# A four-layer attention and Mamba kernel: normed input in both partition halves, the Silu one step later, and layer 1 in half-unit steps

## The chip, the cores and the metric

The kernel runs on one core of a Trainium2 chip, everything in float32. The metric is the device time of one execution in microseconds (us), the median of three runs. The core has a matrix engine (TensorE, PE in the profile, with its weight loads shown apart as PEld), and VectorE (DVE), ScalarE (ACT) and GpSimd (POOL) for elementwise work. SyncE (SP) only issues DMA transfers. Each engine works through its own instructions in program order, and semaphores tie the engines together.

## What is computed

The input is 2 images of 64 channels and 96 x 96 pixels. Four layers follow each other; with two images of 64 channels, the 128 partitions hold image 0 in rows 0 to 63 and image 1 in rows 64 to 127.

- Layer 0 is self-attention over all 9216 pixels, with 1x1 convolutions around it.
- Layer 1 is a depthwise and a 1x1 convolution, then one Mamba block along each image's 9216 pixels as a single sequence.
- Layer 2 is four Mamba blocks: forward and backward along the columns, then forward and backward along the rows, each sequence 96 long.
- Layer 3 is a 3x3 filter whose taps depend on the image's mean.

The change concerns layers 1 and 2. A Mamba block, cut to what matters:

```python
hn = normed(seq)                                  # layer norm (layer 1), RMS norm (layer 2), over 64 channels
xm, z = split(hn @ in_proj_w.T)                   # 64 -> 128 and 128
xc = silu(causal_conv(xm, 4 taps) + convd_b)
dt, Bm, Cm = split(xc @ x_proj_w.T)               # 4, 16, 16
dt = softplus(dt @ dt_proj_w.T + dt_proj_b)
dA = exp(dt[..., None] * A)                       # 128 channels x 16 states
dBx = dt[..., None] * Bm[:, :, None, :] * xc[..., None]
h = h * dA + dBx                                  # along the sequence
y = einsum('bds,bs->bd', h, Cm)
out = ((y + xc * Dp) * silu(z)) @ out_proj_w.T
```

## The kernel before

Work is cut into units of 768 pixels (CH = 768, HALF = 384). Layer 1 has 24 units, 12 per image, one after the other with a carried state; layer 2 has 96, of 8 whole sequences each, a forward and a backward unit sharing one normed input. A unit has 128 channels x 16 states = 2048 recurrences, and they are laid out as 16 groups of 8 channels x 16 states, 128 rows each. So every unit has 16 steps. The rows of dt and of dt*x are written to DRAM and read back, each row repeated, into a tile `spread`.

In layer 1 a step is one group over the whole unit; in layer 2 (`paired`) it is two groups over half of the unit:

```python
    def paired(self, step):
        half, m = divmod(step, self.STEPS // 2)
        return half, (2 * m, 2 * m + 1)
    ...
    def inputs(self, u, step):                     # dt*x*B, VectorE
        if not u.paired:
            u.bx = self.places[0][1]
            self.nc.vector.tensor_mul(u.bx, u.dtu[step][:, CH:], u.B)               # L872
            return
        bx = self.places[step % 2][1].rearrange("p (q t) -> p q t", q=2)
        ...
        B = self.low[0].unsqueeze(1).to_broadcast([P, 2, HALF])
        self.nc.vector.tensor_mul(bx, x, B)                                          # L877

    def scan(self, u, step):                       # VectorE, then GpSimd
        h = u.h[step]
        if not u.paired:
            first = u.carry[:, step : step + 1]
            nc.vector.tensor_tensor_scan(h, h, u.bx, first, ALU.mult, ALU.add)       # L884
            nc.gpsimd.tensor_copy(first, h[:, CH - 1 :])                             # L885
            nc.gpsimd.tensor_mul(h, h, u.C)                                          # L886
            return
        ...
        nc.vector.tensor_tensor_scan(h[:, way], h[:, way], bx[:, way], 0.0, ...)     # L890
        nc.gpsimd.tensor_mul(h, h, C.unsqueeze(1).to_broadcast([P, 2, HALF]))        # L893

    def gather(self, u, step):                     # TensorE: sum over the states, into y
        ...
        if begin:
            ... matmul(p, lhsT=u.w.direct, rhs=u.xc[...], start=True, stop=False)    # L907
        for i, (_, p, q, n) in enumerate(parts):
            ... matmul(p, lhsT=self.t.gather[n], rhs=h[...], start=False, stop=stop) # L910
```

`read` issues the transfer into `spread` five steps ahead (six buffers), `decay` (L853 in layer 1, L857 in layer 2, ScalarE) makes dA three steps ahead, and `shared` (L866, TensorE) puts B of the next unit or half into PSUM: at step 6 for the second half and at step 14 for the next unit. In layer 2, PSUM has one bank for B and one for y, so `y_half` (L915) must copy the first half's sums out at mid-unit before L907 may start the second.

The products of the 64 normed channels use only the rows of one image:

```python
    def conv(self, u, half):                       # L748 in layer 1, L754 in layer 2
        rows = rows_of(u.b)
        x = u.norm.x[rows]
        ...
        for j in range(D_CONV):
            lhsT = u.w.taps[rows, D_CONV - 1 - j]
            ... matmul(p, lhsT=lhsT, rhs=x[:, ...], ...)

    def gate_mm(self, u):
        rows = rows_of(u.b)
        u.p = self.mm([(u.w.gate_w[rows], self.halves(u.norm.x[rows, D_CONV - 1 :]))])

    def gate_read(self, u):
        self.nc.scalar.copy(u.gate, u.p)                                             # L772
        self.nc.scalar.activation(u.raw, u.raw, AF.Silu)                             # L773, with a table load
        self.nc.scalar.preload_act_table_set("natural_log_exp_and_others")           # L774, the load back
```

`mm` is a helper of one line, so that norm, gate, dt, C and output products all stand at L666. Everything apart from the step itself is a piece with an offset in steps relative to its unit; pieces of several units run side by side:

```python
    PIECES = (
        (-51, "norm_centre"), (-49, "norm_square"), (-47, "norm_mean"), (-45, "norm_root"),
        (-38, "norm_scale"), (-36, "norm_affine"),
        (-27, "conv_0"), (-26, "conv_1"), (-25, "conv_read"), (-25, "gate_mm"), (-23, "gate_read"),
        (-21, "step_mm"), (-19, "step_read"), (-18, "step_exp"), (-17, "step_kept"), (-17, "step_log"),
        (-17, "c_mm"), (-15, "c_read"), (-15, "step_sum"), (-11, "step_dt"), (-9, "step_u"), (-8, "step_write"),
        (10, "y_half"), (18, "y_read"), (19, "y_gate"), (25, "tail_0"), (26, "tail_1"), (27, "tail_read"),
    )
```

In each step the main loop gives out: read, decay, inputs and scan, shared, gather of two steps before, then the pieces of that step, those named in `reads` first. `step_kept`, `step_sum`, `step_dt` and `step_u` are products and sums of GpSimd, `step_write` is the transfer of dt and dt*x to DRAM (L824).

Of the kernel before, what the change touches and what calls it, by code (L numbers as in the profile page):

```python
# [25 lines left out]
P = 128  # L26
# [3 lines left out]
NB = 512  # L30
# [41 lines left out]
def setup(ctx, tc, x, cols, mats, dtw):  # L72
# [32 lines left out]
    for b in range(B):  # L105
        nc.vector.memset(k.mean_c[rows_of(b), rows_of(b)], 1.0 / C)
    k.eps = const.tile([P, 1], FP, name="eps")
# [416 lines left out]
def mamba_tables(k, pool):  # L524
# [23 lines left out]
    t.centre = pool.tile([P, P], FP, name="centre")  # L548
    nc.vector.tensor_sub(t.centre, k.ident, k.mean_c)
# [64 lines left out]
class Mamba:  # L614
# [19 lines left out]
    def __init__(self, k, tables, wk, dram, ps, ps_m):  # L634
        self.k, self.nc, self.t = k, k.nc, tables
        self.wk, self.dram, self.ps_m = wk, dram, ps_m


        self.places = [self.wide(ps.tile([P, 2 * NB], FP, name=f"place{i}")) for i in range(2)]
        self.low = [ps.tile([P, NB], FP, name=f"low{i}")[:, :HALF] for i in range(2)]  # L640
# [40 lines left out]

    def norm_centre(self, u):
        if u.carry:
            rows = rows_of(u.b)
            u.p = self.mm([(self.t.centre[rows, rows], self.halves(u.image))], rows)

    def norm_square(self, u):  # L690
        if u.norm.unit is not u:
            return
        rows = rows_of(u.b)
        u.norm.x = self.work("xn", D_CONV - 1 + CH)
        u.sq = self.work("sq", bufs=1)[rows]
        if u.carry:
            self.nc.scalar.activation(u.sq, u.p, AF.Square)
            self.nc.scalar.copy(u.norm.x[rows, D_CONV - 1 :], u.p)
        else:
            n = u.image.shape[1]  # L700
            self.nc.scalar.activation(u.sq.rearrange("p (n t) -> p n t", n=n), u.image, AF.Square)

    def norm_mean(self, u):
        if u.norm.unit is u:
            rows = rows_of(u.b)
            u.p = self.mm([(self.k.mean_c[rows, rows], self.halves(u.sq))], rows)

    def norm_root(self, u):
        if u.norm.unit is u:
            self.nc.scalar.activation(u.sq, u.p, AF.Ln, bias=self.k.eps[rows_of(u.b)])  # L710
            self.nc.scalar.activation(u.sq, u.sq, AF.Exp, scale=-0.5)

    def norm_scale(self, u):
        if u.norm.unit is not u:
            return
        nc, rows = self.nc, rows_of(u.b)
        x = u.norm.x[rows, D_CONV - 1 :]
        if u.carry:
            before = u.norm.x[rows, : D_CONV - 1]
            if u.norm.before is None:  # L720
                nc.gpsimd.memset(before, 0.0)
            else:
                nc.gpsimd.tensor_copy(before, u.norm.before.x[rows, CH:])
            nc.gpsimd.tensor_mul(x, x, u.sq)
        else:
            split = lambda t: t.rearrange("p (n t) -> p n t", n=u.image.shape[1])
            nc.gpsimd.tensor_mul(split(x), u.image, split(u.sq))

    def norm_affine(self, u):
        if u.carry:  # L730
            rows = rows_of(u.b)
            x = u.norm.x[rows, D_CONV - 1 :]
            self.nc.scalar.activation(x, x, AF.Identity, bias=self.k.col("ln_b", rows), scale=self.k.col("ln_g", rows))
# [3 lines left out]
    def conv(self, u, half):  # L737
        rows = rows_of(u.b)
        x = u.norm.x[rows]
        if half == 0:  # L740
            u.sides, u.p = self.open("conv")
        p = u.sides[half]
        c0 = D_CONV - 1 + half * HALF
        for j in range(D_CONV):
            lhsT = u.w.taps[rows, D_CONV - 1 - j]
            flags = dict(start=j == 0, stop=j == D_CONV - 1)
            if u.carry:
                self.nc.tensor.matmul(p, lhsT=lhsT, rhs=x[:, c0 - j : c0 + HALF - j], **flags)  # L748
                continue
            p3 = p.rearrange("p (n t) -> p n t", t=W)  # L750
            x3 = x[:, c0 : c0 + HALF].rearrange("p (n t) -> p n t", t=W)
            late, early = slice(j, W), slice(0, W - j)
            o, i = (early, late) if u.rev else (late, early)
            self.nc.tensor.matmul(p3[:, :, o], lhsT=lhsT, rhs=x3[:, :, i], **flags)  # L754

    def conv_0(self, u):
        self.conv(u, 0)

    def conv_1(self, u):
        self.conv(u, 1)  # L760
# [6 lines left out]
    def gate_mm(self, u):  # L767
        rows = rows_of(u.b)
        u.p = self.mm([(u.w.gate_w[rows], self.halves(u.norm.x[rows, D_CONV - 1 :]))])

    def gate_read(self, u):
        self.nc.scalar.copy(u.gate, u.p)  # L772
        self.nc.scalar.activation(u.raw, u.raw, AF.Silu)  # L773
# [8 lines left out]
    def step_read(self, u):  # L782
# [3 lines left out]
        order = "p (j a t) -> p a j t" if u.paired else "p (a j t) -> p a j t"  # L786
        both = u.both.rearrange(order, a=2, j=2)
# [47 lines left out]
    def paired(self, step):  # L835
        half, m = divmod(step, self.STEPS // 2)
        return half, (2 * m, 2 * m + 1)

    def read(self, u, step):
        u.dtu[step] = self.work("spread", 2 * CH, bufs=6)  # L840
        if not u.paired:
            self.nc.sync.dma_start(out=u.dtu[step], in_=u.rows[8 * step : 8 * step + P])
            return
        half, groups = self.paired(step)
        for q, n in enumerate(groups):
# [3 lines left out]
    def decay(self, u, step):  # L849

        h = u.h[step] = self.work("h", bufs=9)
        if not u.paired:
            self.nc.scalar.activation(h, u.dtu[step][:, :CH], AF.Exp, scale=u.w.rates[:, step : step + 1])  # L853
            return
        for q, n in enumerate(self.paired(step)[1]):
# [3 lines left out]
    def shared(self, u, half=0):  # L859

        if u.paired:
            sides, halves = [self.low[0]], [half]
        else:
            (sides, u.B), halves = self.places[1], range(2)
        for j, p in zip(halves, sides):
            self.nc.tensor.matmul(p, lhsT=u.w.bc[0], rhs=u.xc[:, bass.ts(j, HALF)], start=True, stop=True)  # L866

    def inputs(self, u, step):

        if not u.paired:  # L870
            u.bx = self.places[0][1]
            self.nc.vector.tensor_mul(u.bx, u.dtu[step][:, CH:], u.B)  # L872
            return
        bx = self.places[step % 2][1].rearrange("p (q t) -> p q t", q=2)
        x = u.dtu[step].rearrange("p (q a t) -> p q a t", q=2, a=2)[:, :, 1]
        B = self.low[0].unsqueeze(1).to_broadcast([P, 2, HALF])
        self.nc.vector.tensor_mul(bx, x, B)  # L877

    def scan(self, u, step):
        nc = self.nc  # L880
        h = u.h[step]
        if not u.paired:
            first = u.carry[:, step : step + 1]
            nc.vector.tensor_tensor_scan(h, h, u.bx, first, ALU.mult, ALU.add)  # L884
            nc.gpsimd.tensor_copy(first, h[:, CH - 1 :])  # L885
            nc.gpsimd.tensor_mul(h, h, u.C)  # L886
            return
        bx = self.places[step % 2][1]
        way = slice(None, None, -1) if u.rev else slice(None)
        nc.vector.tensor_tensor_scan(h[:, way], h[:, way], bx[:, way], 0.0, ALU.mult, ALU.add)  # L890
        h = h.rearrange("p (q t) -> p q t", q=2)
        C = u.C[:, bass.ts(self.paired(step)[0], HALF)]
        nc.gpsimd.tensor_mul(h, h, C.unsqueeze(1).to_broadcast([P, 2, HALF]))  # L893

    def gather(self, u, step):

        if u.paired:
            half, groups = self.paired(step)
            parts = [(half, self.low[1], q, n) for q, n in enumerate(groups)]
            begin, end = step % 8 == 0, step % 8 == 7  # L900
        else:
            parts = [(j, p, j, step) for j, p in enumerate(self.low)]
            begin, end = step == 0, step == self.STEPS - 1
        h = u.h[step]
        if begin:
            for half, p in {half: p for half, p, _, _ in parts}.items():
                self.nc.tensor.matmul(p, lhsT=u.w.direct, rhs=u.xc[:, bass.ts(half, HALF)], start=True, stop=False)  # L907
        for i, (_, p, q, n) in enumerate(parts):
            stop = end and (i == 1 or not u.paired)
            self.nc.tensor.matmul(p, lhsT=self.t.gather[n], rhs=h[:, bass.ts(q, HALF)], start=False, stop=stop)  # L910

    def y_half(self, u):
        if u.paired:
            u.y = self.work("yg")
            self.nc.scalar.copy(u.y[:, :HALF], self.low[1])  # L915

    def y_read(self, u):
        if u.paired:
            self.nc.scalar.copy(u.y[:, HALF:], self.low[1])
        elif not u.drained:  # L920
            u.y = self.work("yg")
            for j, p in enumerate(self.low):
                self.nc.scalar.copy(u.y[:, bass.ts(j, HALF)], p)
# [20 lines left out]
    def tail_read(self, u):  # L944
# [19 lines left out]
        (-27, "conv_0"),  # L964
        (-26, "conv_1"),
        (-25, "conv_read"),
        (-25, "gate_mm"),
        (-23, "gate_read"),
        (-21, "step_mm"),
# [20 lines left out]
    def lates(now, s):  # L990
        halves = now and now[0].paired
        if s == 2 or (s == 10 and halves):
            return ()
        if s == 3 or (s == 11 and halves):
            return (3, 2)
        return (2,)

    def run(self, units, first, n_first, other):


        for u in units:
            u.dtu, u.h, u.paired, u.drained = {}, {}, not u.carry, False
        steps = [(u, s) for u in units for s in range(self.STEPS)]
        at = lambda n: steps[n] if 0 <= n < len(steps) else None
        reads = ("norm_square", "norm_root", "conv_read", "gate_read", "step_read", "c_read", "tail_read")

        table = [[] for _ in range(self.STEPS)]
        unit = lambda i: units[i] if i < len(units) else None
# [16 lines left out]
        for n in range(begin, len(steps) + end + 1):  # L1025
# [5 lines left out]
            if at(n):  # L1031
# [3 lines left out]
                if not u.paired:  # L1035
# [318 lines left out]
```

## Time and profile before

| | before |
|---|---|
| time, median of 3 runs | 8185.35 us (8180.19 to 8186.09) |
| span of the profiled execution | 8174.9 us |
| mean granted TensorE clock | 0.955 |
| instructions | 80364 |
| layer 1, first scan to last scan | 2753.5 to 3935.3 us |
| layer 2, first scan to last scan | 3944.0 to 8091.7 us |
| DMA moved | 1725.90 MB |

The first line of the page gives each engine's busy time and its share of the span. A group line gives source line, engine, operation, tile written and tiles read, shapes, count, then busy time and mean nanoseconds of one, then the idle time of that engine just before and what ended most of it. A line of waits names who waited for whom, the total in us, the number of times and the longest. In a timeline each line has the start, the duration, the engine and the source line; square brackets hold the idle time before it. Matmul records come two to a float32 product.

### The profile page before, as it was taken

Reading aid. Unit: us, or ns where it says so; the run is one execution under the profiler, and the core shown is the slowest. Engines: PE = TensorE matmul, PEld = TensorE weight load, DVE = VectorE, ACT = ScalarE, POOL = GpSimd, SP = SyncE. Lnnn points to the kernel's source line nnn. Section 1 sums busy time; section 2 is a strip of 40 time slices with the busy share of each in tenths; the row PEclk is TensorE's granted clock in tenths of the full one; section 3 lists DMA queues with packets and bytes.
Section 4 is the critical chain, followed back from the end, with each engine's and each line's share of the span. In section 5 each row is a group of like instructions: output and inputs, shape, how many; then the busy total and the mean of one; then the engine's idle time right before and its main releaser. Section 6 shows DMA issues by size and latency. Waiting matters only on the chain.

```text
span 8174.9 us, 80364 instructions
## 1 busy us (share of the span) xinstructions
PE 7554.5 (92%) x24578; PEld 3358.0 (41%) x24578; DVE 6785.6 (83%) x5136; ACT 5045.4 (62%) x6473; POOL 4755.1 (58%) x3146
## 2 busy tenths in 40 slices
PE   9999999999999799999889998989999999999897
PEld 3333333333333344444444444444444444444443
DVE  6666666666666599988899999999999999999999
ACT  4444444444444566665676677777777777777774
POOL 0000000000000588888888888898999989888895
PEclk9999999999999798988999999999999999999999
DMA  1000000000000588777888888888898888888885
GB/s 42 1 1 1 1 1 1 3 4 4 4 4 5 205 294 296 284 286 277 292 315 317 317 321 333 330 324 331 334 337 328 330 336 336 331 321 334 324 329 211
DMA packets 538496, 1725.90 MB, mean 211 GB/s; under 512 B 59844, under 2 KB 60996, under 8 KB 537544
## 3 DMA queue, kind: packets, MB, share of 16 engines
q1 hardware_dynamic: 536608, 1717.66, 56.8%
q8 instruction: 194, 3.18, 0.2%
q10 hardware_dynamic: 1448, 3.05, 0.1%
q14 instruction: 246, 2.02, 0.1%
HBM read 1522.68 MB, written 197.79 MB: 210 GB/s over the span
## 4 chain that ended last, share of the span: by engine, by line
PE 21%; POOL 13%; issue 12%; ACT 8%; DMA 8%; DVE 4%; SPq 0%; DVEq 0%; ACTq 0%; POOLq 0%
PE low L910 10%; DMA spread<-rows 6%; POOL h L886 5%; POOL h L893 4%; PE mm L666 4%; ACT h L857 4%; PE conv L754 4%; DVE place L877 2%; DMA rows<-dtu 1%; PE low L907 1%; PE conv L748 1%; DVE h L890 1%; POOL dtu L811 1%; PE low L866 1%; ACT raw L773 1%
## 5 line engine op out<-in xcount | busy, mean ns | idle before, releaser
L910 PE MATMUL low<-h,pair 128*128 128x384 f32 x7680 | 2865.4, 515 | 44.2 <-POOL h L886 26.5
L893 POOL TENSOR_TENSOR h<-h,C 128x768 f32<-128x768 f32 x1536 | 2755.1, 1819 | 231.7 <-DVE h L890 225.1
L890 DVE TENSOR_TENSOR_SCAN h<-h,place 128x768 f32<-128x768 f32 x1536 | 2604.3, 1737 | 4.9 <-ACT h L857 4.9
L910 PEld LDWEIGHTS low<-h,pair 128*128 128x128 f32 x7680 | 1503.2, 201 | 1288.6 <-issue 270.7
L307 ACT ACTIVATE e<-f_exp 128x1536 f32<-128x1536 f32 x864 | 1207.1, 1449 | 1223.7 <-PE f_exp L297 1223.7
L363 DVE TENSOR_TENSOR acc_e<-acc_e,e 128x1536 f32<-128x1536 f32 x792 | 1389.9, 1755 | 684.5 <-ACT e L307 645.2
L857 ACT ACTIVATE h<-spread,xa 128x384 f32<-128x384 f32 x3072 | 1717.2, 607 | 368.7 <-DMA spread<-rows 336.8
L877 DVE TENSOR_TENSOR place<-spread,low 128x768 f32<-128x768 f32 x1536 | 1388.3, 949 | 251.0 <-PE low L866 238.4
L336 POOL TENSOR_TENSOR xa<-xa,t_att 64x512 f32<-64x512 f32 x36 | 45.4, 1261 | 2612.4 <-ACT t_att L334 2612.4
L314 PE MATMUL y_att<-e,xb 128*64 128x512 f32 x5184 | 1243.6, 601 | 0.0
L297 PE MATMUL f_exp<-theta,phi 64*128 64x512 f32 x5184 | 1234.4, 606 | 1.0 <-DVE xb L280 0.5
L297 PEld LDWEIGHTS f_exp<-theta,phi 64*128 64x128 f32 x5184 | 466.2, 186 | 754.6 <-issue 460.8
L884 DVE TENSOR_TENSOR_SCAN h<-h,state,place 128x768 f32<-128x768 f32 x384 | 696.1, 1813 | 67.7 <-ACT h L853 19.2
L886 POOL TENSOR_TENSOR h<-h,C 128x768 f32<-128x768 f32 x384 | 695.3, 1811 | 31.4 <-POOL state L885 1.0
L314 PEld LDWEIGHTS y_att<-e,xb 128*64 128x64 f32 x5184 | 341.5, 136 | 830.7 <-issue 829.3
L765 ACT ACTIVATE raw<-conv,cols 128x768 f32<-128x768 f32 x120 | 108.2, 901 | 886.1 <-PE conv L754 587.0
L754 PE MATMUL conv<-xn,xa 64*128 64x384 f32 (+3 forms) x1536 | 557.9, 503 | 16.6 <-DVE xa L1128 5.3
L872 DVE TENSOR_TENSOR place<-spread,place 128x768 f32<-128x768 f32 x384 | 369.1, 961 | 129.3 <-PE place L866 116.9
L853 ACT ACTIVATE h<-spread,rates 128x768 f32<-128x768 f32 x384 | 351.1, 931 | 175.0 <-DMA spread<-rows 173.6
L907 PE MATMUL low<-raw,xa 128*128 128x384 f32 x384 | 220.2, 662 | 257.8 <-ACT yg L915 175.6
L754 PEld LDWEIGHTS conv<-xn,xa 64*128 64x128 f32 x1536 | 277.6, 190 | 286.7 <-issue 98.7
L805 POOL TENSOR_TENSOR kept<-dtu,kept 128x768 f32<-128x768 f32 x120 | 218.2, 1819 | 285.1 <-ACT kept L798 285.1
(207 smaller groups left out, 6041.4 us busy)
## 6 DMA issues: line engine op xcount, KB each, us to landing
spread<-rows SPq DMA_DIRECT2D x3072, 384.0 KB, 6.4
spread<-rows SPq DMA_DIRECT2D x384, 768.0 KB, 4.5
rows<-dtu SPq DMA_DIRECT2D x240, 768.0 KB, 5.8
image<-pre SPq DMA_DIRECT2D x11, 384.0 KB, 2.3
xb<-image SPq DMA_DIRECT2D x11, 384.0 KB, 7.9
xa<-in_x SPq DMA_DIRECT2D x1, 2304.0 KB, 22.2
out<-xa ACTq DMA_DIRECT2D x7, 240.0 KB, 2.0
out<-xa SPq DMA_DIRECT2D x1, 1200.0 KB
```

Source lines behind the costliest of these rows:

```text
L297: nc.tensor.matmul(fs[j // 3][:, bass.ts(j % 3, NB)], lhsT=phi[at, bass.ts(m // 2, P)], rhs=theta[at, bass.ts(i, NB)], start=True, stop=True,)
L307: nc.scalar.activation(e, f, AF.Exp)
L314: nc.tensor.matmul(y[rows_of(m % 2)], lhsT=g[:, m, :], rhs=es[j // 3][:, bass.ts(j % 3, NB)], start=m < 2, stop=m >= KEYS - 2,)
L363: nc.vector.tensor_add(acc, acc, e)
L754: self.nc.tensor.matmul(p3[:, :, o], lhsT=lhsT, rhs=x3[:, :, i], **flags)
L857: self.nc.scalar.activation(h[:, bass.ts(q, HALF)], dt, AF.Exp, scale=u.w.rates[:, n : n + 1])
L877: self.nc.vector.tensor_mul(bx, x, B)
L884: nc.vector.tensor_tensor_scan(h, h, u.bx, first, ALU.mult, ALU.add)
L886: nc.gpsimd.tensor_mul(h, h, u.C)
L890: nc.vector.tensor_tensor_scan(h[:, way], h[:, way], bx[:, way], 0.0, ALU.mult, ALU.add)
L893: nc.gpsimd.tensor_mul(h, h, C.unsqueeze(1).to_broadcast([P, 2, HALF]))
L910: self.nc.tensor.matmul(p, lhsT=self.t.gather[n], rhs=h[:, bass.ts(q, HALF)], start=False, stop=stop)
```

## The change

The normed input, until now in the 64 rows of its own image, is made twice, in rows 0 to 63 and 64 to 127. With that, a product over 64 rows can take the first half of the unit from the lower rows and the second half from the upper ones, so that the two sides lie next to each other in the array's rows, each in its own PSUM bank. This concerns the mean, the conv and the gate. Second, the Silu with its two table loads becomes a piece of its own, one step after the gate's copy, and `y_half` moves to the front of its step. Third, layer 1 takes the half-unit steps of layer 2: two groups over half of the unit, each scan cut in two because the two groups have different carried states. The branches on `paired` go away.

```diff
-    t.centre = pool.tile([P, P], FP, name="centre")
-    nc.vector.tensor_sub(t.centre, k.ident, k.mean_c)
+    t.centre = pool.tile([P, 2, C], FP, name="centre")
+    for j in range(2):
+        nc.vector.tensor_add(t.centre[:, j], k.ident[:, :C], k.ident[:, C:])
+        nc.vector.tensor_scalar_add(t.centre[:, j], t.centre[:, j], -1.0 / C)
...
-        self.low = [ps.tile([P, NB], FP, name=f"low{i}")[:, :HALF] for i in range(2)]
+        self.B, self.y = [ps.tile([P, NB], FP, name=name)[:, :HALF] for name in ("B", "y")]
...
+    def mm_split(self, lhsT, rhs):
+        sides, whole = self.open()
+        for j, p in enumerate(sides):
+            at = rows_of(j)
+            self.nc.tensor.matmul(p, lhsT=lhsT[at], rhs=rhs[at, bass.ts(j, HALF)], start=True, stop=True)
+        return whole
...
     def norm_centre(self, u):
         if u.carry:
-            u.p = self.mm([(self.t.centre[rows, rows], self.halves(u.image))], rows)
+            u.p = self.mm([(self.t.centre[rows_of(u.b)], self.halves(u.image))])
...
     def norm_square(self, u):
...
         else:
-            n = u.image.shape[1]
-            self.nc.scalar.activation(u.sq.rearrange("p (n t) -> p n t", n=n), u.image, AF.Square)
+            for j in range(2):
+                self.nc.scalar.copy(x[rows_of(j)].rearrange("p (n t) -> p n t", n=u.image.shape[1]), u.image)
+            self.nc.scalar.activation(u.sq, x, AF.Square)
...
-            u.p = self.mm([(self.k.mean_c[rows, rows], self.halves(u.sq))], rows)
+            u.p = self.mm_split(self.k.mean, u.sq)
...
-    def conv(self, u, half):
...
+    def conv(self, u):
+        sides, u.p = self.open("conv")
         for j in range(D_CONV):
...
+            for half, p in enumerate(sides):
+                at = rows_of(half)
+                x, lhsT = u.norm.x[at], u.w.taps[at, D_CONV - 1 - j]
...
     def gate_mm(self, u):
-        u.p = self.mm([(u.w.gate_w[rows], self.halves(u.norm.x[rows, D_CONV - 1 :]))])
+        u.p = self.mm_split(u.w.gate_w, u.norm.x[:, D_CONV - 1 :])
 
     def gate_read(self, u):
         self.nc.scalar.copy(u.gate, u.p)
+
+    def silu(self, u):
         self.nc.scalar.activation(u.raw, u.raw, AF.Silu)
         self.nc.scalar.preload_act_table_set("natural_log_exp_and_others")
...
     def scan(self, u, step):
...
+        half, turns = self.turns(step)
+        h, bx = u.h[step], self.places[step % 2][1]
+        h2 = h.rearrange("p (q t) -> p q t", q=2)
+        if u.carry:
+            state = u.carry[:, turns[0] : turns[1] + 1]
+            for q in range(2):
+                at = bass.ts(q, HALF)
+                nc.vector.tensor_tensor_scan(h[:, at], h[:, at], bx[:, at], state[:, q : q + 1], ALU.mult, ALU.add)
+            nc.gpsimd.tensor_copy(state.unsqueeze(2), h2[:, :, HALF - 1 :])
+        else:
...
+        nc.gpsimd.tensor_mul(h2, h2, u.C[:, bass.ts(half, HALF)].unsqueeze(1).to_broadcast([P, 2, HALF]))
...
-        (-27, "conv_0"),
-        (-26, "conv_1"),
+        (-27, "conv"),
         (-25, "conv_read"),
         (-25, "gate_mm"),
         (-23, "gate_read"),
+        (-22, "silu"),
         (-21, "step_mm"),
...
-        reads = ("norm_square", "norm_root", "conv_read", "gate_read", "step_read", "c_read", "tail_read")
+        reads = ("y_half", "norm_square", "norm_root", "conv_read", "gate_read", "step_read", "c_read", "tail_read")
```

The cut parts are the other side of each `paired` branch, the same rows in `norm_scale` and `norm_affine`, and the main loop without its cases for layer 1. The 1x1 products, the attention of layer 0 and layer 3 stay as they are.

## The prediction

> **What bounds the kernel now.** I read the page first, then the waits, then the timeline of VectorE (DVE) in the middle of layer 2, then the busy time by stretch. The page shows no single full engine:
>
> ```profile
> PE 7554.5 (92%) x24578; PEld 3358.0 (41%) x24578; DVE 6785.6 (83%) x5136; ACT 5045.4 (62%) x6473; POOL 4755.1 (58%) x3146
> ```
>
> That is an average over four stages. The scans tell the stages apart: L884 (layer 1) first starts at 2753.5 us, L890 (layer 2) runs from 3944.0 to 8091.7 us. So attention takes 2.65 ms, layer 1 (24 units of 16 steps) 1190 us or 49.6 us a unit, layer 2 (96 units) 4149 us or 43.2 us a unit, and the end 82 us. The diff leaves attention and layer 3 alone, so only 5.34 ms can move. The costliest groups there:
>
> ```profile
> L910 PE MATMUL low<-h,pair 128*128 128x384 f32 x7680 | 2865.4, 515 | 44.2 <-POOL h L886 26.5
> L893 POOL TENSOR_TENSOR h<-h,C 128x768 f32<-128x768 f32 x1536 | 2755.1, 1819 | 231.7 <-DVE h L890 225.1
> L890 DVE TENSOR_TENSOR_SCAN h<-h,place 128x768 f32<-128x768 f32 x1536 | 2604.3, 1737 | 4.9 <-ACT h L857 4.9
> ...
> L877 DVE TENSOR_TENSOR place<-spread,low 128x768 f32<-128x768 f32 x1536 | 1388.3, 949 | 251.0 <-PE low L866 238.4
> ```
>
> DVE never waits for its scan, but it waits 251 us before the products L877, nearly all of it for L866, the two matmuls that put the next B in PSUM. The DVE timeline shows what it does when nothing holds it, and what one hold costs:
>
> ```profile
> 5005.81 3.39 DVE L890 TENSOR_TENSOR_SCAN h<-h,place 128x768 f32<-128x768 f32 x2
> 5012.80 1.83 DVE L877 TENSOR_TENSOR place<-spread,low 128x768 f32<-128x768 f32 x2 [3.60 <-PE low L866]
> 5014.54 3.39 DVE L890 TENSOR_TENSOR_SCAN h<-h,place 128x768 f32<-128x768 f32 x2
> 5017.85 1.80 DVE L877 TENSOR_TENSOR place<-spread,low 128x768 f32<-128x768 f32 x2
> 5019.56 3.39 DVE L890 TENSOR_TENSOR_SCAN h<-h,place 128x768 f32<-128x768 f32 x2
> ```
>
> From scan pair to scan pair is 5014.54 to 5019.56, 5.02 us for two steps, so a unit can't be shorter than 8 x 5.02 = 40.1 us, while it takes 43.2. Why is L866 late? PE takes its matmuls in order, and the waits show what stands ahead of it:
>
> ```profile
> DVE place L877 <- PE low L866: 238.4, 99, 5.2
> ...
> PEld low L907 <- ACT yg L915: 205.8, 49, 4.3
> PE low L907 <- ACT yg L915: 175.6, 49, 3.7
> ```
>
> L915 is y_half, ScalarE's copy that empties the single y bank at mid-unit; L907 is the first matmul into it afterwards. In the whole timeline L774 (the second table load of the Silu) runs 4999.16 to 5000.44, two decays follow, y_half runs at 5001.48, and L907 starts at 5001.99 after PE idled 3.71 us. PE then works without a break until L866 at 5011.96. The Silu block on ScalarE (load 1.28, Silu 1.48, load 1.28 = 4.04 us) therefore reaches DVE through PE. PE cannot catch up soon, as it is nearly full, and so are the others:
>
> ```profile
> 6000.00:7000.00 1000.00, 908.18 (x2526) 467.02 (x2526) 944.71 (x750) 724.33 (x1136) 900.65 (x529) 0.95 0.89 333
> 7000.00:8000.00 1000.00, 906.15 (x2511) 463.93 (x2509) 937.86 (x746) 722.64 (x1124) 892.17 (x524) 0.95 0.88 328
> ```
>
> (Columns: PE, weight loads, DVE, ACT, POOL busy; clock; DMA share; GB/s.) Per unit of 43.2 us: PE 39.2, DVE 40.7, ACT 31.3, POOL 38.7, DMA 38.2.
>
> **What the skill says.** "TensorEngine Tiling (Array Packing)", section Key Properties: different tiles of the array can load and multiply at the same time, and a change of the tiling mode drains the array. This trace agrees with the first: attention's 64-row scores L297, which alternate between the row halves, cost 1234.4/5184 = 238 ns for 512 columns, 0.47 ns a column, against 2865.4/7680 = 373 ns for 384 columns, 0.97 ns a column, for full-height L910. The timeline also shows some 0.55 us of PE idle where it turns to a 64-row product. "TensorE: Matmul & The Clock Gate", section The mechanism (what overlaps): matmuls keep program order, which is what the chain above needs. "ScalarE: Activation LUTs", section What ACT_TABLE_LOAD costs: 1283 ns and a drain of some 1380 ns. The load is 1283 ns here as well, but Silu follows it at once (5038.71 plus 1.28, next start 5040.01), so I count no drain.
>
> **The change part by part.**
>
> *Side-by-side products.* The conv L754 is 16 matmul records a unit, 557.9/96 = 5.8 us. Its two sides now sit in different row halves and different banks, alternately in program order; by the L297 ratio that halves: 2.9 us saved. The gate (192.0 us for 120 units, 1.6 us each) saves 0.8; the mean (121.9 us for 72 norms, 1.7 us each) saves 0.85 per norm, 0.4 per layer 2 unit. Sum 4.1 us of PE per unit, 39.2 to 35.1. In layer 1 the conv L748 costs 190.5/24 = 7.9, so 4.0 + 0.8 + 0.85 = 5.6 us.
>
> *Both halves filled.* In layer 2 one strided 64-row Square (1198 ns) becomes two such copies (my estimate 1.2 us each, same shape) and a plain Square (0.8): +2.0 us of ACT per norm, 1.0 per unit. Off the path unless ACT is late there. POOL's norm product goes from 1997 to about 1820 ns: nothing.
>
> *Silu a step later, y_half ahead of the rest of its step.* The 4.04 us block now lies behind y_half, so PE's 3.7 us wait shrinks to what the gathers themselves cause. Nothing is saved on ACT; the wait moves to step_mm, which needs the Silu, one step of 2.5 us later. In between PE has L907 and two steps of gathers, so I expect that wait near zero.
>
> *Sum for layer 2.* With 4.1 us less to do and 3.7 us less to wait in half of the units, PE is ready before DVE asks. The 238 us of L866 waits go. Floor: 96 x 40.1 = 3850 us. Layer 2's first half also holds DVE work for the weights of later nets, about 30 us by the groups outside L877/L890. I add 0.5 us a unit for the rivals below: 3850 + 30 + 48 = 3928, against 4149: **221 us saved**.
>
> *Layer 1 in half-unit steps.* Now a step is a product of 0.96 and a scan of 1.81, start to start 2.94, as each product waits for the scan before it (one buffer): 47 us a unit of the 49.6. After: two products in 1.71 us (as in layer 2), then four scans of 384 elements. A 768-scan costs 1.66 start to start, [...]so 384 is about 0.86, and L884 with its state operand is 0.08 longer than L890, giving 0.94; if it does not overlap, 1.03. Pair: 1.71 + 4 x 0.94 = 5.5 to 1.71 + 4 x 1.03 = 5.8 us; unit 44 to 46.6. POOL: per step 1.81 plus the state copy and gaps, 2.06, so 33.0, plus five products of 1.8 and a norm, 43.8 us. Two limits at 44 to 46; with weights' work and stalls I take 46.8 a unit, 1123 us against 1190: **67 us saved**.
>
> *Before the first scan.* The first two units run alone in a chain: conv 9.1 and 10.6 us, gate 2.9 twice, mean 2.8 twice. Halved that is 15 us at most; I take **10**.
>
> Sum: 8185 - 221 - 67 - 10 = 7887, say 7890.
>
> **Rivals.** (1) *POOL takes over.* 38.7 of 40.1 us leaves 1.4 us, and POOL now waits 285 us over 120 units, 2.4 each, for ACT's `kept`. For: ACT waits for DMA just there. Against: those waits come partly from step_mm being late behind the PE stall, and a POOL that runs later waits less. If the wait stays in full a unit takes 41.1, layer 2 loses another 50 us and layer 1 perhaps 25: 7960.
> (2) *DMA takes over.* 38.2 us of busy DMA in 40.1 is 95%, and the queue's own waits show it cannot run evenly:
>
> ```profile
> SPq L824 <- POOL dtu L819: 736.1, 95, 10.0
> ```
>
> Every unit the write of dt and u holds up the reads behind it for 7.7 us. ACT waits 337 us for these reads already, without passing it on (L890 waits 4.9 us). If it is passed on, 41.5 to 42 us a unit: about 8000.
> (3) *The halves don't run side by side*, or mode changes eat it: only the Silu move and layer 1 remain, half the layer 2 gain: about 8000.
> (4) *Four short scans cost more than I think*: layer 1 stays at 1190: 7955.
> A slowdown would need two of these and layer 1 losing outright.
>
> **Range and chances.** 2% is 164 us, so 8021 is the line; each rival alone stays under it. All waits vanishing and layer 1 at 44.5 gives about 7800. Range 7800 to 8020. Faster 0.87, same 0.10, slower 0.03.
>
> **What would show it.** Conv records near 0.19 us of busy time instead of 0.36; waits of L907 for y_half and of L877 for L866 mostly gone; DVE in layer 2 at 97% busy or more, units near 40.5 us; POOL and DMA shares near 0.95; layer 1 at 45 to 47 us a unit, its scans near 1.0 us long. It is wrong if DVE waits instead for ACT's decays (rival 2), if POOL's products lag by several steps (rival 1), or if step_mm's wait for the later Silu makes L866 late as before.

## The result and the profile after

The changed kernel takes 7977.4 us (7973.19 to 7985.06) against 8185.72 us (8180.19 to 8191.08): ratio 0.9747, 95% interval 0.973 to 0.9763. It is 208 us faster, where 295 were predicted. The sum came near for partly wrong reasons: layer 1 gave more than expected, layer 2 about a third.

First the whole page, the engines' busy time and the conv's group:

```profile
PE 7063.0 (89%) x24578; PEld 3122.4 (39%) x24578; DVE 6749.1 (85%) x5524; ACT 5214.3 (65%) x6953; POOL 4724.4 (59%) x3146
...
L761 PE MATMUL conv<-xn,xa 64*128 64x384 f32 (+3 forms) x1536 | 273.1, 494 | 11.7 <-DVE xa L1093 4.0
```

TensorE has 491 us less to do. The conv of layer 2 costs 273.1/1536 = 178 ns a record where it cost 363: the halves do run side by side. The mean of 494 ns is the duration of one record, almost unchanged; two of them now overlap.

Now the stretches of the two layers, first the kernel before, then the changed one (columns: stretch, length, then PE, PEld, DVE, ACT, POOL busy, clock, DMA share, GB/s):

```profile
2753.00:3944.00 1191.00, 1093.31 (x2824) 517.45 (x2822) 1076.73 (x802) 747.30 (x867) 1008.50 (x932) 0.91 0.78 286
3944.00:8093.00 4149.00, 3744.54 (x10329) 1907.48 (x10328) 3894.26 (x3108) 2980.05 (x4595) 3679.31 (x2151) 0.95 0.88 327
```

```profile
2734.00:3822.00 1088.00, 938.11 (x2812) 459.35 (x2813) 1041.79 (x1184) 818.02 (x1248) 995.43 (x932) 0.95 0.85 311
3822.00:7893.00 4071.00, 3431.68 (x10344) 1738.47 (x10342) 3891.40 (x3108) 3080.64 (x4695) 3662.65 (x2153) 0.95 0.89 333
```

Layer 1 lost 102 us, what lies before it 19, layer 2 only 78, of which 221 were expected. DVE's work in layer 2 is the same 3890 us, and the 255 us of loss on top of it became 180. The waits inside layer 2, before and after, tell where the loss now is (who waits, for whom; us in total, times, longest):

```profile
DVE place L877 <- PE low L866: 233.2, 98, 4.4
...
PE low L907 <- ACT yg L915: 175.6, 49, 3.7
...
PE mm L666 <- ACT C L831: 100.9, 46, 3.7
...
PE low L907 <- ACT yg L919: 82.1, 49, 5.5
```

```profile
PE y L885 <- ACT yg L895: 182.8, 74, 5.2
...
PE mm L693 <- ACT C L832: 163.2, 46, 5.5
DVE place L863 <- PE B L857: 137.1, 84, 3.2
...
PE mm L671 <- ACT xb L924: 91.5, 46, 4.0
...
PE y L885 <- ACT yg L892: 27.7, 48, 1.0
```

TensorE's wait for y_half (L915, now L892) fell from 176 to 28 us, as predicted. In its place TensorE waits for other things that ScalarE does in its order: for y_read (L895, 82 before, 183 now), for C's copy that frees the PSUM buffer of the norm's mean (L832, 101 and 163), and for tail_read, which frees it for step_mm (L924). So B is still late, for 137 us. One case, ScalarE in the changed kernel and then TensorE:

```profile
6515.50 1.66 ACT L714 COPY xn<-xb 64x768 f32<-64x768 f32 x2
6517.19 0.84 ACT L715 ACTIVATE sq<-xn 128x768 f32<-128x768 f32 x1
6517.94 0.83 ACT L803 ACTIVATE log<-dtu 128x768 f32<-128x768 f32 x1
6518.67 2.12 ACT L853 ACTIVATE h<-spread,xa 128x384 f32<-128x384 f32 x4
6520.70 0.78 ACT L832 COPY C<-mm 128x768 f32<-128x768 f32 x1
```

```profile
6521.53 0.92 PE L693 MATMUL mm<-sq,mean 64*128 64x384 f32 x4 [2.17 <-ACT C L832]
6522.91 0.92 PE L885 MATMUL y<-raw,xa 128*128 128x384 f32 x2 [0.47 <-ACT yg L895]
```

The two new copies L714 stand ahead of C's copy in ScalarE's order, and TensorE idles 2.17 us for it. Later in the unit B for the second half comes 1.17 us late on DVE:

```profile
6534.30 1.83 DVE L863 TENSOR_TENSOR place<-spread,B 128x768 f32<-128x768 f32 x2 [1.17 <-PE B L857]
```

### The profile page after: what moved, and what is told of

Its sections match the earlier page's. It is cut to its first block, busy times and chain, and to the rows that moved or that the text cites. A ratio compares the mean times of both kernels' runs of the same rounds, so it can differ in the third digit from the quotient of the medians.

```text
span 7974.9 us, 82275 instructions
## 1 busy us (share of the span) xinstructions
PE 7063.0 (89%) x24578; PEld 3122.4 (39%) x24578; DVE 6749.1 (85%) x5524; ACT 5214.3 (65%) x6953; POOL 4724.4 (59%) x3146
## 4 chain that ended last, share of the span: by engine, by line
PE 11%; DMA 10%; ACT 9%; issue 8%; POOL 8%; DVE 4%; SPq 1%; DVEq 0%; ACTq 0%; POOLq 0%
DMA spread<-rows 7%; PE y L888 6%; POOL h L879 6%; ACT h L853 3%; DMA rows<-dtu 3%; PE mm L671 2%; DVE place L863 2%; DVE h L878 1%; PE conv L761 1%; POOL dtu L812 1%; POOL dtu L816 1%; PE y L885 1%; DVE xa L1211 1%; ACT xn L714 1%; PE mm L693 1%
## 5 line engine op out<-in xcount | busy, mean ns | idle before, releaser
L888 PE MATMUL y<-h,pair 128*128 128x384 f32 x7680 | 2809.6, 510 | 103.4 <-POOL h L879 102.7
L888 PEld LDWEIGHTS y<-h,pair 128*128 128x128 f32 x7680 | 1513.6, 200 | 1306.8 <-POOL h L879 239.6
L863 DVE TENSOR_TENSOR place<-spread,B 128x768 f32<-128x768 f32 x1920 | 1735.0, 948 | 261.9 <-PE B L857 250.8
L874 DVE TENSOR_TENSOR_SCAN h<-h,state,place 128x384 f32<-128x384 f32 x768 | 714.0, 990 | 0.0
L853 ACT ACTIVATE h<-spread,rates 128x384 f32<-128x384 f32 x768 | 433.0, 608 | 150.3 <-DMA spread<-rows 137.5
L885 PE MATMUL y<-raw,xa 128*128 128x384 f32 x384 | 220.4, 663 | 210.5 <-ACT yg L895 182.8
L671 PE MATMUL mm<-raw,xa 128*128 128x384 f32 x768 | 301.2, 517 | 99.2 <-ACT xb L924 91.5
L761 PE MATMUL conv<-xn,xa 64*128 64x384 f32 (+3 forms) x1536 | 273.1, 494 | 11.7 <-DVE xa L1093 4.0
L892 ACT COPY yg<-y 128x384 f32<-128x384 f32 x120 | 57.4, 478 | 289.7 <-PE mm L671 205.1
L857 PE MATMUL B<-raw,xa 128*128 128x384 f32 x384 | 170.7, 526 | 83.8 <-DVE place L863 83.7
```

What stands on the lines that cost most here:

```text
L671: self.nc.tensor.matmul(o, lhsT=lhsT, rhs=x, start=n == 0, stop=n == len(terms) - 1)
L853: self.nc.scalar.activation(h[:, bass.ts(q, HALF)], dt, AF.Exp, scale=u.w.rates[:, n : n + 1])
L863: self.nc.vector.tensor_mul(bx, x, self.B.unsqueeze(1).to_broadcast([P, 2, HALF]))
L874: nc.vector.tensor_tensor_scan(h[:, at], h[:, at], bx[:, at], state[:, q : q + 1], ALU.mult, ALU.add)
L888: self.nc.tensor.matmul(self.y, lhsT=self.t.gather[n], rhs=rhs, start=False, stop=stop)
```

## The experiments

Three theories for the missing part. **A**: TensorE, lighter now, is held by ScalarE's program order. **B**: DMA, at 0.89 of its 16 engines, is the limit. **C**: GpSimd is. Two more formed on the way: **D**, reads come late because SyncE holds them behind a write, and that makes ScalarE late; **E**, the copies are the cost. Times of layer 2 below run from its first to its last scan: 4147.7 us in the kernel before, 4069.1 in the changed one. Times of layer 1 run from its first scan to the first of layer 2. They are read from one trace of each kernel, and executions of one kernel differ by up to 30 us here, so that differences of a few us mean nothing.

**The Silu put back** (silu_back).

```diff
     def gate_read(self, u):
         self.nc.scalar.copy(u.gate, u.p)
+        self.silu(u)
-        (-22, "silu"),
```

> The changed kernel with the Silu and its two table loads back in the gate's read (step 9), y_half still at the front of step 10. Theory A (what is left of layer 2's loss is TensorE waiting for ScalarE in program order): y_half stands behind the 4.0 us block again, TensorE waits for it at L885 some 2 to 4 us a unit, layer 2 goes from 42.4 to 43 us a unit, total 8030 to 8070. Rival B (DMA at 0.89 of 16 engines is the limit) and rival C (GpSimd at 0.90 is): no more than 15 us of difference, 7965 to 7990.

7981.4 us, ratio 0.9754 (0.9737 to 0.9771); layer 2 4071.4. No difference from the changed kernel. TensorE waits for y_half again (86 us in the second half of layer 2 alone), but less for y_read. Theory A in this form, that the Silu's place matters, missed; B and C had the number right.

**Both sides in one row half** (no_side).

```diff
-            at = rows_of(j)
+            at = rows_of(0)
...
-                at = rows_of(half)
+                at = rows_of(0)
```

> The changed kernel, but both sides of the mean, the conv and the gate take the rows 0 to 63, so that they follow each other in one row half; everything else, the copies into both halves too, is unchanged, and so is what is computed. TensorE gets some 4.1 us a unit more work in layer 2 and 5.6 in layer 1. Theory A: layer 2 goes back to about 44 us a unit (+150 us), layer 1 to 46.5 (+25), total 8120 to 8180. Rivals B and C: TensorE was not the limit, total under 8010.

8254.5 us, ratio 1.009 (1.0071 to 1.011): slower than the kernel before, and by more than any theory had. Layer 2 is 4317.6, so the side-by-side products are worth 249 us there; in layer 1 next to nothing (1097 us against 1089). The loss of the rest of the change in layer 2, +170 us against the kernel before, was a surprise and led to the last runs.

**A third yg buffer** (yg3).

```diff
-        u.y = self.work("yg")
+        u.y = self.work("yg", bufs=3)
-        u.sq = self.work("sq", bufs=1)
+        u.sq = self.sq                      # in a free part of xa
```

> The changed kernel with a third buffer for yg (the squares move to a free part of xa to make room), so that y_half of a unit after a pair need not wait for the tail that still reads the old buffer. Theory A: ScalarE's wait at y_half (205 us for a product L671 in the trace of the changed kernel) falls under 60 us, the Silu and tail_read come some 3 us earlier in every second unit, and the stall of VectorE at the end of these units (slot 15: 4.6 instead of 3.35 us) shrinks: 40 to 65 us less, 7910 to 7940. Rivals B and C: 7965 to 7990.

7970.2 us, ratio 0.9738 (0.9721 to 0.9755): 7 us, no difference that the intervals can tell, and far from theory A's 40 to 65. The wait of y_half for the tail is gone from the list of waits, as meant, but it turned into another wait of ScalarE, for its reads, which rose from 481 to 622 us in the whole run. That put the reads under suspicion.

**The copies earlier** (copy_early).

```diff
+    def norm_copy(self, u):
+        ...                                 # the two copies, out of norm_square
+        (-57, "norm_copy"),
         (-51, "norm_centre"),
+    # xn: bufs=3; u.sq in a free part of xa
```

> The changed kernel with the two copies of layer 2's input moved from step 15 to step 7 of the same unit, ahead of conv_read, where ScalarE waits for the conv anyway (xn gets a third buffer, the squares move to a free part of xa). Theory A: c_read and y_read come 1.7 to 2.4 us earlier, TensorE's wait of norm_mean for C (170 us) falls under 100, and the stall at half of the other units (slot 7: 4.8 instead of 3.35 us) shrinks: 40 to 70 us less, 7905 to 7940. Rivals B and C: 7965 to 7990.

7950.2 us, ratio 0.9714 (0.9697 to 0.9731): 27 us, a part of what was expected. TensorE's wait of the mean for C fell as meant, from 163 us in layer 2 to 56. All of the gain is in layer 2's first half (2036.6 against 2064.8 us), where the copies read strided rows (1479 ns each, against 827 in the second half). What the third buffer of xn gave by itself was not tested.

**The write on another queue** (write_act).

```diff
-            self.nc.sync.dma_start(out=u.rows[j * P : (j + 1) * P], in_=u.both)
+            self.nc.scalar.dma_start(out=u.rows[j * P : (j + 1) * P], in_=u.both)
-        (-8, "step_write"),
         (10, "y_half"),
+        (-6, "step_write"),
...
-        reads = ("y_half", ...
+        reads = ("step_write", "y_half", ...
```

> The changed kernel with the write of dt and dt*x issued by ScalarE behind y_half (step 10) instead of by SyncE at step 8. Theory D: reads stand on SyncE behind a write that waits for GpSimd, come late, and ScalarE, waiting for them in its decays, reaches tail_read, C's copy and y_read late, which holds TensorE and then B. Then SyncE's wait at the write (some 7 us a unit) is gone, ScalarE's wait for spread falls from 481 us under 300, and layer 2 loses 50 to 100 us: 7880 to 7930. Theory A (ScalarE's own order and load alone): 7960 to 7990.

7918.8 us, ratio 0.9679 (0.9663 to 0.9695): 58 us. Of the two lines of SyncE's waits in the changed kernel that stand for the held write,

```profile
SPq L825 <- POOL dtu L820: 705.0, 95, 9.0
...
SPq L825 <- POOL state L875: 190.7, 24, 8.6
```

none is left. Layer 1 goes from 1088.6 to 1044.0 us, with DVE busy 99.6% of it: its floor. Layer 2 gains only 25, where theory D gave it 50 to 100: the total lies in D's range because of layer 1, which D did not name (the first scan comes 13 us later in this run). ScalarE's wait for reads fell to 436 us and not under 300, so its sum is a poor sign here. The Trainium skill, "Trainium Kernel Development and Optimization", section Key Constraints, has it that issuing DMAs from several engines only saves the sequencer's issue time; here it saved 58 us, as the sequencer's time was in large part a wait, 7.4 us a unit with reads behind it. The run also puts the write two steps later, and the two are not told apart.

**Half of the bytes** (half_dma; layer 2 takes dt in place of dt*x and has no reset, so its output is another).

```diff
-            nc.gpsimd.memset(u.dt.rearrange(...)[:, :, :, first : first + 1], 1e30)
+            nc.gpsimd.memset(u.dt.rearrange(...)[:, :, :, first : first + 1], 1.0)
...
+            n = CH if u.carry else HALF
-            self.nc.sync.dma_start(out=u.dtu[step][:, bass.ts(q, CH)], in_=row)
+            self.nc.sync.dma_start(out=u.dtu[step][:, q * CH : q * CH + n], in_=row[:, :n])
-        x = u.dtu[step].rearrange("p (q a t) -> p q a t", q=2, a=2)[:, :, 1]
+        x = u.dtu[step].rearrange("p (q a t) -> p q a t", q=2, a=2)[:, :, 1 if u.carry else 0]
```

> The changed kernel, but layer 2 reads only dt, half of the bytes in the same number of transfers, and takes dt in place of dt*x in its products (and no reset at the sequence starts), so the output differs; engines have the same work. Theory D and rival B (bytes of DMA): ScalarE no longer waits for spread in layer 2 and the units go to 40.3 to 41 us: 7800 to 7860. Theory A: 7950 to 7990.

7907.2 us, ratio 0.966 (0.9644 to 0.9676): layer 2 4001.6, 67 us less, and above the 7800 to 7860 of D and B. This line is layer 2 of that run:

```profile
3819.00:7823.00 4004.00, 3388.09 (x10339) 1688.01 (x10338) 3885.71 (x3108) 3006.97 (x4691) 3663.85 (x2154) 0.97 0.59 188
```

DMA at 0.59 instead of 0.89 leaves 118 us of DVE idle. So bytes are not the limit: with half of them gone, 67 of the 180 us go, and a later run with all of them has a shorter layer 2 (write_copy, 3973.4).

**GpSimd with less work** (pool_less; the output lacks a rounding correction).

```diff
     def step_kept(self, u):
-        self.nc.gpsimd.tensor_sub(u.kept, u.e, u.kept)
+        pass
```

> The changed kernel without the subtraction step_kept on GpSimd (1.8 us a unit and its wait for ScalarE; the output loses a rounding correction). Rival C (GpSimd at 0.90 is the limit): 1 to 1.8 us a unit, 100 to 200 us less, 7780 to 7880. Theory A: 7960 to 7990. Theory D: up to 40 us less, because dt*x is ready earlier and SyncE is held up less, 7935 to 7980.

7957.6 us, ratio 0.9718 (0.9702 to 0.9734): 20 us for 218 us of work removed, where the intervals of this run and the changed kernel just touch. C falls; D's small gain fits, as dt*x can be ready earlier.

**Silu and y_half alone, in the kernel before** (before_silu).

```diff
         (-23, "gate_read"),
+        (-22, "silu"),
-        reads = ("norm_square", ...
+        reads = ("y_half", "norm_square", ...
```

> The kernel before with the Silu as a piece of its own one step later and y_half at the front of its step, nothing else. By the prediction TensorE's wait of 176 us for y_half goes and with it a part of the wait for B: 8060 to 8110. If the wait only moves to step_mm and tail_read, as the run with the Silu put back suggests: 8150 to 8195.

8234.2 us, ratio 1.0052 (1.0032 to 1.0071): slower by 46 us, which no theory had. Layer 2 goes from 4147.7 to 4200.0. Its trace has less waiting of DVE for B (145 us) but new waits for ScalarE's decays (97 us, where it was 5) and for reads (47 us, where it was 12).

**Only the new order undone** (both_back: Silu and y_half in their old places).

```diff
     def gate_read(self, u):
         self.nc.scalar.copy(u.gate, u.p)
+        self.silu(u)
-        (-22, "silu"),
-        reads = ("y_half", "norm_square", ...
+        reads = ("norm_square", ...
```

> The changed kernel with Silu and y_half both in their old places. As Silu and y_half moved alone made the kernel before 46 us slower and Silu put back alone changed nothing, the order of y_half would be what costs: 7930 to 7960. If the new order is worth what the prediction gave it: 8030 to 8070. If it does not matter once the products lie side by side: 7965 to 7990.

7983.5 us, ratio 0.9763 (0.9747 to 0.978), layer 2 4070.4: with the products side by side the new order is worth nothing.

**The new order undone, and no side by side** (no_side_back).

```diff
     # the edits of both_back, and
-            at = rows_of(j)
+            at = rows_of(0)
...
-                at = rows_of(half)
+                at = rows_of(0)
```

> The changed kernel with the products in one row half and with Silu and y_half in their old places: what remains of the change is layer 1 in half-unit steps and the input normed into both halves (the copies). Layers 1 and before as in the run without side by side (2756 and 1097 us), the end 82. Theory E (the copies on ScalarE, 1.7 us per norm more in the second half of layer 2 and 2.4 in the first, reach VectorE through TensorE): layer 2 over the 4149 us of before by 40 to 120, total 8125 to 8205. If the copies are off the path, as the prediction had it: layer 2 at 4149, total 8075 to 8095.

8231.0 us, ratio 1.0064 (1.0047 to 1.0081), layer 2 4299.2. What remains of the change there made layer 2 151 us slower, above the expected 40 to 120.

**The conv in two pieces again** (copies_only), so that layer 2 has only the norm into both halves left.

```diff
     # the edits of no_side_back, and
-    def conv(self, u):
+    def conv(self, u, which):               # one side of the unit at a time
...
-        (-27, "conv"),
+        (-27, "conv_0"),
+        (-26, "conv_1"),
```

> The run before last but one (products in one row half, Silu and y_half in their old places) with the conv in two pieces again, one on each side of B's product for the second half, as in the kernel before. In layer 2 only the norm into both halves is then left of the change; layer 1 stays in half-unit steps (2752 and 1100 us before and in it). If the copies made layer 2's 4301 us there: it stays over 4260, total 8190 to 8235. If the conv in one piece ahead of B did, layer 2 returns to 4149 to 4180, total 8080 to 8115. From the slots I expect both: half of the 152 us each, layer 2 at 4200 to 4250, total 8130 to 8185.

8227.9 us, ratio 1.0058 (1.0041 to 1.0076), layer 2 4306.1: not the mixture I expected; the norm into both halves makes all of it, 158 us. The time from first scan to first scan places it. Every second unit, the one that has the mean of a norm in its second step with the Square two steps earlier, went from 44.5 to 48.4 us in layer 2's first half and from 45.4 to 48.2 in its second; the units between them stayed at 42.9 and at 40.4 to 40.5. The waits in its layer 2, against those of before above:

```profile
DVE place L872 <- PE B L866: 354.2, 120, 5.2
...
PE mm L693 <- ACT C L841: 189.8, 46, 5.1
```

B is late for 354 instead of 233 us, and the mean waits for C for 190 instead of 101. That is 1.9 us more for each of the 46 norms counted, close to what the copies add on ScalarE (2 x 1185 ns and 844 against 1198: 2.0 us), so theory E fits. The mean's product with 128 output rows instead of 64 and GpSimd's product (1543 ns instead of 1989) are in the 158 us too; no run takes the copies alone.

A norm costs 3.3 us, though, not 2.0. By the trace, the rest is TensorE running slower. This is layer 2 of copies_only, to be read against the line of the kernel before above:

```profile
3833.00:8141.00 4308.00, 3819.74 (x10347) 1951.73 (x10345) 3896.59 (x3108) 3046.28 (x4694) 3661.48 (x2153) 0.93 0.85 315
```

TensorE idles 84 us more, and its products take 75 us more; together 159. One place in both kernels, first before, then copies_only:

```profile
6516.87 1.50 PE L666 MATMUL mm<-sq,mean_c 64*64 64x384 f32 x4 [1.99 <-ACT C L831]
6518.30 0.91 PE L907 MATMUL low<-raw,xa 128*128 128x384 f32 x2
6519.05 5.32 PE L910 MATMUL low<-h,pair 128*128 128x384 f32 x16
```

```profile
6517.81 2.92 PE L693 MATMUL mm<-sq,mean 64*128 64x384 f32 x4 [3.75 <-ACT C L841]
6520.66 1.65 PE L894 MATMUL y<-raw,xa 128*128 128x384 f32 x2
6522.10 5.97 PE L897 MATMUL y<-h,pair 128*128 128x384 f32 x16
```

After 1.99 us of idling the granted clock was 1.00 (6516.8 to 6519.0 us); after 3.75 us it was 0.50 (6517.8 to 6522.0 us), and the same products took nearly twice as long. In layer 2 of copies_only a stretch at half clock began during, or within 1.5 us after, 89 of the 93 pauses of TensorE of 3.5 us or more, and 5 of the 62 pauses of 1 to 3.5 us; in all 597 us of the layer ran at half clock, 420 in the kernel before. So the copies lengthened a wait of some 2 us to some 4, and the longer wait also slowed the work behind it. This is read from the traces; no run sets the clock apart.

**Both improvements together** (write_copy: write_act and copy_early).

```diff
-            self.nc.sync.dma_start(out=u.rows[j * P : (j + 1) * P], in_=u.both)
+            self.nc.scalar.dma_start(out=u.rows[j * P : (j + 1) * P], in_=u.both)
+        (-57, "norm_copy"),
-        (-8, "step_write"),
+        (-6, "step_write"),
```

> The changed kernel with the write of dt and dt*x on ScalarE's queue and the copies in step 7. The two runs alone gave 58 and 27 us; if they are two separate delays the sum: 7880 to 7905. If both only shorten the same wait: 7915 to 7925.

7829.8 us, ratio 0.9572 (0.9556 to 0.9588): 148 us faster than the changed kernel, more than the sum of 58 and 27 and outside both expectations. Its two layers:

```profile
2740.00:3784.00 1044.00, 924.63 (x2818) 441.92 (x2818) 1039.44 (x1183) 819.48 (x1248) 994.29 (x931) 0.98 0.91 325
3784.00:7759.00 3975.00, 3403.12 (x10337) 1694.53 (x10335) 3885.65 (x3108) 3091.88 (x4692) 3660.39 (x2153) 0.97 0.93 341
```

With the write out of the way, moving the copies gives 71 us of layer 2 (4044.2 to 3973.4) instead of 29; with the copies out of the way, moving the write gives 67 instead of 25. So each had hidden part of the other. That either delay alone was enough to make ScalarE late is my reading, not traced. The time at half clock in layer 2 also fell, from 423 us in the changed kernel to 249, and no run tells how much of the gain is that. The kernel also moves more bytes per second than the changed kernel, which speaks against B once more.

## Why the prediction was right, and where it was not

Layer 2, by the differences between runs (first to last scan). In layer 2 each pair differs in the step named; the first row is the whole norm into both halves, not the copies alone. The sizes hold for this order of the steps: in other company, side by side gave -249 (no_side) and the new order +52 (before_silu) or +18 (no_side against no_side_back).

| step | predicted | measured | from |
|---|---|---|---|
| both halves filled | 0, off the path | +158 | before, copies_only |
| conv in one piece | not considered | -7 | copies_only, no_side_back |
| side by side | 4.1 us of TensorE a unit | -229 | no_side_back, both_back |
| Silu later, y_half first | a 3.7 us wait less | -1 | both_back, changed kernel |
| sum | -221 | -79 | |

That the sum is not further off is in part luck: side by side alone gave what was expected of the whole layer, and a loss of 158 us that the prediction had put at 0 took most of it back. Moving the copies and the write (write_copy) brings layer 2 to 3973.4, 96 us of the 142 that were missing.

**What bounds it.** Right: DVE's pace of 5.02 us for two steps is the floor, its work stayed at 3890 us, and B coming late through a nearly full TensorE was the loss. Overlooked: after the 3.71 us that TensorE idled at L907 in the prediction's timeline, the granted clock was 0.53 (5002 to 5008 us), and eight products L910 took 4.82 us at 5003.43 where eight took 2.74 at 5009.38. Of the signs named, conv records (178 ns), L907's wait (28 us), the layer 1 scans (989 ns) and units (45.4 us) came; in layer 2 DVE was busy 95.6% and not 97, a unit took 42.4 us and not 40.5, and GpSimd and DMA stood at 0.90 and 0.89 and not near 0.95.

**Side-by-side products.** Right in mechanism, and for the conv in size: 178 ns a record where 190 was given. The gate (110.0 us instead of 192.0) and the mean (84.5 instead of 121.9) fell by less than half. Worth 229 to 249 us, as much as the prediction gave to all of layer 2. The 0.55 us at a turn to a 64-row product was misread: it is idle time of the weight loads (PEld), while the matmuls themselves start 0.42 us apart there instead of 0.32.

**The Silu.** The wait for y_half went, and step_mm's wait for the Silu stayed near zero (7.4 us) as expected. What failed is "PE is ready before DVE asks": TensorE waited instead for tail_read (91 us, at step_mm, for its PSUM buffer) and y_read (183 us). I took the wait on the chain for the cause. By the waits, moving the 4 us block changed which of ScalarE's results came late; putting it back in the changed kernel changed nothing, and moving it in the kernel before made that 46 us slower.

**Both halves filled.** The failed step. 2.0 us of ScalarE per norm was well sized, and "off the path unless ACT is late there" was the mistake: ScalarE was late exactly there. A line of the profile before said so, TensorE's wait of 101 us for C; I did not read it.

**Layer 1.** Predicted 67, measured 102 us. The mechanism held, and the scans were over-sized. The timeline of the changed kernel:

```profile
3007.55 3.72 DVE L874 TENSOR_TENSOR_SCAN h<-h,state,place 128x384 f32<-128x384 f32 x4
3011.19 1.80 DVE L863 TENSOR_TENSOR place<-spread,B 128x768 f32<-128x768 f32 x2
3012.90 3.72 DVE L874 TENSOR_TENSOR_SCAN h<-h,state,place 128x384 f32<-128x384 f32 x4
```

A pair of steps takes 3012.90 - 3007.55 = 5.35 us, under the 5.5 to 5.8 given, as four scans need 3.64 us to the next product; a unit takes 45.4 us instead of 46.8. The pace accounts for the whole gain: 16 x 2.94 = 47.0 us a unit before, 8 x 5.35 = 42.8 now, 4.2 us in 24 units. In copies_only layer 1 is as fast without side by side (1080 us), so this gain does not come from side by side; it comes with the half-unit steps.

**Before the first scan.** 19 us instead of 10; the runs with side by side begin it at 2734 to 2747 us, those without at 2752 to 2768.

**Rivals.** POOL (1) is not the limit: 20 us for its lighter run. DMA (2) is not by its bytes, but its held write is a part of it, 58 us alone, most of it in layer 1. (3) and (4) did not happen. What stays open is the 87 us that DVE still waits for B in layer 2 of write_copy (51 times), where TensorE waits 188 us for y_read. The half clock alone does not decide either: silu_back spends 553 us of layer 2 at it, the changed kernel 423, and they take the same time.

## What to carry to other kernels

When several engines are over 85% busy, ask of every instruction added, even to the idlest, what stands behind it in that engine's order and who waits for that: here 2 us of ScalarE per norm, with the engine 28% idle, came with 158 us in layer 2 while the products still stood one after the other. Look too at what a longer wait does afterwards: TensorE's busy time for the same products rose with its idle time. A wait on the chain need not be the cause; undo each part alone before crediting it. And delays that hide each other must be removed together before the gain of either can be seen.

## What was not expected of the hardware

A scan of 384 elements with its start value from memory followed the one before in 0.91 us, and one of 768 in 1.66, so two halves cost 2 x 0.91 - 1.66 = 0.16 us more than one whole scan. And two 64-row products in different row halves cost no more than one: 178 ns against 363 a record. The granted clock of TensorE fell to one half after pauses of 3.5 us and more (89 of 93 in layer 2 of copies_only).
